# A threshold search on VectorE: one count with a sum, or a compare and a second compare that adds and sums

## The chip, the cores and the metric

The kernel runs on one core of a Trainium2 chip. The metric is device time in microseconds (us) of one execution; lower is better. The engines are named as the profile names them: PE is TensorE, DVE is VectorE, ACT is ScalarE, POOL is GpSimd, SP is SyncE.

## What is computed

One layer of a perceiver on 16 x 64 = 1024 tokens of width 1024: cross attention to 1601 context rows per batch entry, a gated feed-forward block that keeps only the larger half of its gate activations, and a small mixture of experts. The part that matters here is the middle one:

```python
def _L0_attn_ref(x, w_gate, w_up, w_down):
    s = jax.nn.silu(jnp.einsum('bsh,ih->bsi', x, w_gate))
    B, S, I = s.shape                       # I = 2752
    k = int(K_FACTOR * I)                   # 1376
    _, idx = jax.lax.top_k(-jnp.abs(s), k)
    flat = s.reshape(B * S, I)
    rows = jnp.arange(B * S)[:, None]
    flat = flat.at[rows, idx.reshape(B * S, k)].set(0.0)
    s = flat.reshape(B, S, I)
    s = s * jnp.einsum('bsh,ih->bsi', x, w_up)
    return jnp.einsum('bsi,hi->bsh', s, w_down)
...
x = x + _L0_xattn_ref(_layernorm(x, axis=-1), ctx_1024, ctx_1024, 0, mask_SxS2_ff0)
x = x + _L0_attn_ref(_layernorm(x, axis=-1), L0_attn_w_gate, L0_attn_w_up, L0_attn_w_down)
x = x + _L0_ffn_ref(_layernorm(x, axis=-1), ...)
```

In every token's row of 2752 gate values the 1376 of least magnitude are set to zero, the earliest ones where magnitudes are equal.

## The kernel before

The 1024 tokens are eight tiles of 128 rows (partitions). Attention comes first and takes about half of the time. GpSimd uses it to form sums of weight blocks for the feed-forward block, whose three matrix products are done for two tiles at a time, in a form with seven block products in place of eight (Strassen's way).

The feed-forward block works on four pairs of tiles. For pair n there is a gate projection (`widen` with k = 0, group g0 to g3), an up projection (`widen` with k = 1, u0 to u3) and a down projection (`down`, d0 to d3). Each unit of `widen` is eight PE matmuls into one of five PSUM banks; DVE and ACT add the products out of PSUM (evictions), and for the up projection POOL multiplies the result into the gate's rows `s` (tiles `v_u` in the profile). In `down`, POOL forms the sums of blocks of `s` that the seven products need (`S<-s`, `s<-s,s`, `s<-S,s`).

Between gate and down projection stands the selection, `drop_small`. It takes the magnitudes `a[0]` and `a[1]` of the pair's two tiles and finds for each row, bit by bit from bit 30 down, the threshold below which 1376 values lie. A float's bits, for positive numbers, order like the number, so the candidate threshold is built as an integer. Each of the 31 steps has three tasks:

- `below`, on DVE: for tile 0 of the pair, how many of 2752 magnitudes are under the candidate, less 1376, into `over[:, 0]`. It is one instruction, a compare whose accumulator starts at -1376. Its elementwise output `junk0` (2752 bytes a row) is not used in the search.
- `signs`, on ACT: for tile 1 of the pair, the sum of the signs of candidate minus magnitude, into `over[:, 1]`.
- `settle`, on DVE: two instructions on 128 x 2 values, `marks` and `cand`, which take the tried bit back where at least 1376 values were under it, and set the next.

After the last step come the ranks of equal values (a compare into `junk0`, then a scan, per half row and tile), the mask (`keep`, a three-operand instruction written into `rank`) and, on POOL, the multiplication of `s` by the mask (`zero`, in the profile `s<-s,rank`, 128 x 688). It needs the up projection's columns as well. Then PE turns the rows (`turned`, in the profile `ptd`) and the down projection starts. The magnitudes of the next pair are formed only when the pair before is done with `a`, so the four searches follow one another; and the up projection of a pair starts only when that pair's magnitudes exist.

The order of all this work is fixed when the program is built. Every piece is a task of `Plan`, with an engine, a cost in us, its dependences, a rank and the buffers that it takes. `Plan.run` plays the tasks in time with these costs and 0.1 us for a result that goes to another engine; whenever an engine is free it emits the ready task of lowest rank. The instructions of each engine then run in that order on the chip, whatever the real durations are. A task's cost is thus no limit on the chip, but it moves tasks of all engines in the order. The ranks of the projections on PE follow

```python
    order = ["g0", "u0", "g1", "g2", "d0", "u1", "g3", "d1", "u2", "d2", "u3", "d3"]
```

and in the search `below` and `signs` have rank 3, `settle` 1, evictions 0. Each step's tasks depend on the step before:

```python
            t0 = add("DVE", 3.15, below, [t], 3)
            t1 = add("ACT", 2.8, signs, [t], 3)
            t = add("DVE", 0.35, settle, [t0, t1], 1)
```

All recorded instructions carry the line of a helper (L93 in the profile), so the profile's groups are told apart by the names of tiles.

Of the kernel before, what the change touches and what calls it, by code (L numbers as in the profile page):

```python
# [9 lines left out]
F32 = mybir.dt.float32  # L10
I32 = mybir.dt.int32
BF16 = mybir.dt.bfloat16
# [4 lines left out]
ALU = mybir.AluOpType  # L17
# [13 lines left out]
I = 2752  # L31
# [11 lines left out]
WC = 3 * HC  # L43
GW, DW = NCC * (NH // 2) * IC, NB * HC
NU = 16
assert I % 2 == 0
K_ZERO = I // 2
E, R = 8, 16
SCALING = 8.0 / R
EPS = 1e-5  # L50
# [4 lines left out]
def tile_perceiver_layer(  # L55
# [41 lines left out]
    pe, dve, act = InOrder(nc.tensor), InOrder(nc.vector), InOrder(nc.scalar)  # L97
# [264 lines left out]
    def finish_tile(i, h, home=ps_t, tag="pt"):  # L362


        if h == 0:
            att[i] = xnp.tile([P, 2, 4, 4, HD], F32, tag="xn", name=f"att{i}")
        rows = att[i][:, h]
        pt = home.tile([P, 4, P], F32, tag=tag, name=f"pto{i}_{h}")
        for r in range(4):
            pe.transpose(  # L370
                pt[:, r, :], oT[i][:, h, r].rearrange("p b s -> p (b s)"), ident
            )

        def add():
            pool.tensor_tensor(
                rows, rows, rs_tok[i][:, h].unsqueeze(3).to_broadcast([P, 4, 4, HD]),
                ALU.mult,
            )
            xv = x[i].rearrange("p (h g r d) -> p h r g d", h=2, g=4, r=4)
            pool.tensor_tensor(xv[:, h], xv[:, h], rows, ALU.add)  # L380

        return (rows, pt.rearrange("p r (g d) -> p r g d", g=4)), add
# [35 lines left out]
    for n in range(ng):  # L418
# [11 lines left out]
        for d in range(2):  # L430
            add = None
# [6 lines left out]
            if n > 8 and 3 <= 2 * m + d <= 4:  # L438
                copy, add = finish_tile(i - 2, 1 - d)
# [93 lines left out]
    add = plan.add  # L533
    s, hS, held_h, hs, a, marked = {}, {}, {}, {}, {}, {0: [], 1: []}
# [232 lines left out]
    def drop_small(pair, n, gated, after, up):  # L767
# [10 lines left out]
        box = {}  # L778
# [18 lines left out]
        t = add("DVE", 4.4, magnitudes, gated[pair[0]] + gated[pair[1]] + after, 1)  # L797
        upped = up([t])
        for bit in range(30, -1, -1):

            def below():
                dve.tensor_scalar(
                    box["junk0"], a[0], box["cand"][:, 0:1].bitcast(F32),
                    float(-K_ZERO), ALU.is_lt, ALU.add,
                    accum_out=box["over"][:, 0:1],
                )

            def signs():
                act.activation(
                    box["sign1"], a[1], AF.Sign, bias=box["cand"][:, 1:2].bitcast(F32),  # L810
                    scale=-1.0, accum_out=box["over"][:, 1:2],
                )

            def settle(bit=bit):

                gone = marks[:, 2 * bit : 2 * bit + 2]
                dve.tensor_scalar(
                    gone, box["over"], 0.0, float(1 << bit), ALU.is_ge, ALU.mult
                )
                cand = small.tile([P, 2], I32, tag="cand", name=f"cand{n}_{bit}")  # L820
                dve.scalar_tensor_tensor(
                    cand, box["cand"], (1 << bit) >> 1, gone,
                    ALU.bitwise_or, ALU.bitwise_xor,
                )
                box["cand"] = cand
                box["over"] = small.tile([P, 2], F32, tag="over", name=f"over{n}_{bit}")

            t0 = add("DVE", 3.15, below, [t], 3)
            t1 = add("ACT", 2.8, signs, [t], 3)
            t = add("DVE", 0.35, settle, [t0, t1], 1)  # L830

# [15 lines left out]
        def one_short():  # L847
# [3 lines left out]
            dve.tensor_scalar(  # L851
                step, box["unequal"], box["trial"], float(2 * (I - K_ZERO)),
                ALU.subtract, ALU.is_gt,
# [11 lines left out]
        for j, i in enumerate(pair):  # L865
# [33 lines left out]
            t = [t] + [ts1] * j + marked[j]  # L899
            for h in range(2):  # L900
                t = [add("DVE", 5.5 if j else 4.0, lambda h=h, f=ranks: f(h), t, 2)]
            t = add("DVE", 0.6, limits, t + [tb[j]], 2)
            for h in range(2):
                t = add("DVE", 1.75, lambda h=h, f=keep: f(h), [t], 2)
# [334 lines left out]
    t = add("PE", 2.9, lambda: groups[-1].values(0, NTC), [], rank["g0"] - 5)  # L1239
    t = add("ACT", 0.3, lambda: groups[-1].keep(), [t], 0)  # L1240
# [23 lines left out]
    t = add("DVE", 1.3, sum_blocks, [over], rank["g1"], margin=30.0)  # L1264
    t = add("PE", 0.25, sum_rows, [t], rank["g0"], takes=held_ra)
# [4 lines left out]
    for n, pair in enumerate(pairs):  # L1270
        kept, t = drop_small(
            pair, n, gated[n], chosen,
            lambda t: widen(1, n, pair, rank[f"u{n}"], f"u{n}", lambda p: t, t),
        )
        chosen = [t]
        turns = turned(pair, rank[f"d{n}"] - 1, kept)
        downed = down(pair, n, rank[f"d{n}"], turns)
        for i in pair:
            ends[i] = experts(i, downed[i])
        if n == 0:  # L1280
            gated.append(
                gate(pairs[3], 3, rank["g3"], lambda i: ends[i - 6])
            )
# [3 lines left out]
class Plan:  # L1287
# [20 lines left out]
    def add(self, engine, cost, emit, deps, rank, takes=None, frees=None, margin=0.0):  # L1308
        holds, frees = (
            [hold for hold in (h if isinstance(h, tuple) else (h,)) if hold]  # L1310
            for h in (takes, frees)
        )
        task = self.Task(engine, cost, emit, deps, rank, holds, margin)
        for hold in frees:
            hold.freed_by = task
        self.tasks.append(task)
        return task
# [98 lines left out]
```

## Time and profile before

| what | value |
|---|---|
| three runs | 1718.9, 1718.66 and 1722.92 us, median 1718.9 |
| profiled execution, span from first to last instruction | 1719.5 us (no time of it outside the span is recorded) |
| PE busy | 1694.0 us, 99% of the span |
| DVE busy | 1413.0 us, 82% |
| ACT busy | 1259.6 us, 73% |
| POOL busy | 557.2 us, 32% |
| mean granted PE clock | 0.995 |
| `below` (junk<-a,cand, 128 x 2752) | 124 instances, mean 3078 ns, 381.7 us |
| `signs` (sign<-a,cand, 128 x 2752) | 136 instances (12 outside the steps), mean 2587 ns, 351.9 us |
| `marks` and `cand` of `settle` | 124 each, 157 ns |
| the four searches, first count to last settle | 920.9 to 1053.9, 1093.6 to 1228.7, 1271.2 to 1399.4, 1448.0 to 1579.8 us |

A line of the profile's groups names the engine, the operation, output <- inputs by the program's names, the shapes, how many instances there are, and their times. A timeline's line begins with the start and the duration in us; brackets at its end give the time for which the engine was idle before it and what ended that. Engines run beside each other, so busy shares do not add up.

### The profile page before, as it was taken

The page shows a single profiled execution, that of the slowest core. Times are in us where ns is not written, and L with a number is a line of the kernel's source. Part 1 is how long each engine was busy: PE and PEld are TensorE (multiplying, and loading weights), DVE is VectorE, ACT ScalarE, POOL GpSimd, SP SyncE. Part 2 cuts the span into 40 slices and gives each one's busy share as a digit, 9 for nine tenths or more (in the row PEclk, how much of TensorE's full clock was granted, in tenths as well). Part 3 has the DMA queues.
Part 4 walks back from the last instruction along what each step waited for, and adds up shares of the span by engine and source line. Part 5 has one row for each costly group of instructions (what it writes and reads, how often), then busy time and mean ns, then how long its engine had stood idle before and what let it go on. Part 6 is the DMA issues. An engine that isn't in the chain of part 4 may idle for free. (4 is left out here: it accounts for less than half of the span.)

```text
span 1719.5 us, 38732 instructions
## 1 busy us (share of the span) xinstructions
PE 1694.0 (99%) x15102; PEld 1152.2 (67%) x15102; DVE 1413.0 (82%) x3655; ACT 1259.6 (73%) x1780; POOL 557.2 (32%) x584
## 2 busy tenths in 40 slices
PE   8999999999999999999999999999989999999999
PEld 6777777777777777777766666655645646645644
DVE  7888888888888888888627999999999989999703
ACT  5999999999999999999544676577657782778010
POOL 2045454454444454110120211222282013331631
PEclk9999999999999999999999999999999999999999
DMA  8246456555556646121499999988969978888984
GB/s 248 74 122 207 148 194 210 188 166 195 170 185 206 204 159 208 57 75 58 182 349 324 308 292 304 302 267 291 324 202 292 309 251 301 283 294 270 316 265 143
DMA packets 132327, 384.56 MB, mean 224 GB/s; under 512 B 9489, under 2 KB 61233, under 8 KB 132145
## 3 DMA queue, kind: packets, MB, share of 16 engines
q1 hardware_dynamic: 113280, 312.83, 55.5%
q0 software_dynamic: 18432, 68.16, 12.1%
q8 instruction: 120, 1.97, 0.5%
q10 hardware_dynamic: 432, 1.09, 0.2%
q14 instruction: 63, 0.51, 0.1%
HBM read 339.58 MB, written 42.47 MB: 222 GB/s over the span
## 5 line engine op out<-in xcount | busy, mean ns | idle before, releaser
L93 DVE CUSTOM_DVE_ANT_0 sc<-ps,mask 128x512 f32<-128x512 f32 (+2 forms) x1024 | 526.4, 571 | 104.8 <-PE ps L93 104.4
L93 ACT ACTIVATE sign<-a,cand 128x2752 int8<-128x2752 f32 x136 | 351.9, 2587 | 110.9 <-DVE cand L93 110.5
L93 ACT ACTIVATE sc<-sc,nm 128x1601 f32<-128x1601 f32 x256 | 420.2, 1667 | 11.5 <-DVE nm L93 11.5
L93 PEld LDWEIGHTS pt<-ident,sc 128*128 128x128 f32 (+1 forms) x3328 | 361.9, 141 | 77.3 <-issue 72.8
L93 PE MATMUL pt<-ident,sc 128*128 128x128 f32 (+1 forms) x3328 | 391.1, 274 | 1.0 <-ACT sc L93 0.9
L93 DVE TENSOR_SCALAR_CACHE_REDUCE junk<-a,cand 128x2752 uint8<-128x2752 f32 x124 | 381.7, 3078 | 4.0
L93 ACT COPY pT<-pt 128x512 f32<-128x512 f32 x636 | 323.9, 609 | 46.5 <-PE pt L93 46.2
L93 PE MATMUL pg_g<-w_g,hS 128*128 128x344 f32 x896 | 261.2, 453 | 2.6 <-DMA w_g<-ts 1.8
L93 PE MATMUL pg_u<-w_u,hS 128*128 128x344 f32 x896 | 263.4, 452 | 0.0
L93 POOL TENSOR_TENSOR tw<-tw 128x344 f32<-128x344 f32 (+1 forms) x192 | 175.9, 927 | 265.5 <-DMA tw<-in_wg_dram 87.3
L93 PE MATMUL ps<-kT,qt 32*128 32x512 f32 (+2 forms) x2048 | 248.1, 550 | 4.6 <-DMA kT<-in_ctx_t_dram 3.4
L93 PE MATMUL pd<-w_d,s 128*128 128x512 f32 x528 | 235.2, 599 | 0.0
L93 PEld LDWEIGHTS pg_g<-w_g,hS 128*128 128x128 f32 x896 | 169.5, 190 | 91.0 <-issue 3.3
L93 PEld LDWEIGHTS pg_u<-w_u,hS 128*128 128x128 f32 x896 | 168.8, 190 | 87.4 <-issue 3.4
L93 PE MATMUL po<-pT,v 128*32 128x128 f32 x6656 | 208.2, 274 | 0.4 <-ACT oT L93 0.4
L93 PEld LDWEIGHTS po<-pT,v 128*32 128x32 f32 x6656 | 174.1, 110 | 48.6 <-issue 45.7
L93 PEld LDWEIGHTS pd<-w_d,s 128*128 128x128 f32 x528 | 99.9, 193 | 115.7 <-issue 114.6
L93 DVE COPY pT<-pt 65x128 f32<-65x128 f32 (+1 forms) x388 | 141.0, 418 | 22.9 <-PE pt L93 16.0
L93 PEld LDWEIGHTS ps<-kT,qt 32*128 32x128 f32 x2048 | 83.3, 184 | 53.9 <-DVE mx L93 36.7
L93 ACT ACTIVATE s<-s 128x344 f32<-128x344 f32 (+1 forms) x70 | 36.6, 535 | 74.8 <-DVE s L93 74.7
L93 POOL TENSOR_TENSOR s<-s,rank 128x688 f32<-128x688 f32 x32 | 62.4, 1965 | 77.3 <-DVE rank L93 76.7
L93 DVE DVE_READ_ACCUMULATOR2_ANT mx<- 128x1 f32 x1024 | 84.0, 82 | 0.0
(322 smaller groups left out, 1216.6 us busy)
## 6 DMA issues: line engine op xcount, KB each, us to landing
w_g<-ts SPq DMA_DIRECT2D x64, 688.0 KB
w_u<-ts SPq DMA_DIRECT2D x64, 688.0 KB
w_d<-ts SPq DMA_DIRECT2D x48, 768.0 KB
w_g<-in_wg_dram SPq DMA_DIRECT2D x48, 688.0 KB
w_u<-in_wu_dram SPq DMA_DIRECT2D x48, 688.0 KB
w_d<-in_wd_dram SPq DMA_DIRECT2D x36, 768.0 KB
kT<-in_ctx_t_dram SPq DMA_DIRECT2D x31, 800.5 KB
v<-in_ctx_v_dram SPq DMA_DIRECT2D x32, 768.0 KB
```

The costliest lines, as they stand in the source:

```text
L93: return tc.keep_in_program_order(getattr(self.engine, op)(*args, **kwargs))
```

## The change

The count of `below` becomes two instructions. The first compares the upper 1376 columns of `a[0]` with the candidate and adds -1, so that it writes 0 or -1 for each; it writes 16-bit values (the same bytes `junk0`, seen as 1376 values of bf16) and has no sum. The second compares the lower 1376 columns, adds the first one's output element by element, and sums: the sum is the number of magnitudes under the candidate less 1376, as before. The cost that `Plan` reckons for the task goes from 3.15 to 2.65. The rest of the search, `signs` and `settle` among it, stays.

```diff
-assert I % 2 == 0
 K_ZERO = I // 2
+assert K_ZERO == I - I // 2
...
         for bit in range(30, -1, -1):
 
             def below():
+                half, cand = I // 2, box["cand"][:, 0:1].bitcast(F32)
+                less = box["junk0"].bitcast(BF16)
                 dve.tensor_scalar(
-                    box["junk0"], a[0], box["cand"][:, 0:1].bitcast(F32),
-                    float(-K_ZERO), ALU.is_lt, ALU.add,
+                    less, a[0][:, half:], cand, -1.0, ALU.is_lt, ALU.add
+                )
+                dve.scalar_tensor_tensor(
+                    less, a[0][:, :half], cand, less, ALU.is_lt, ALU.add,
                     accum_out=box["over"][:, 0:1],
                 )
...
-            t0 = add("DVE", 3.15, below, [t], 3)
+            t0 = add("DVE", 2.65, below, [t], 3)
             t1 = add("ACT", 2.8, signs, [t], 3)
             t = add("DVE", 0.35, settle, [t0, t1], 1)
```

## The prediction

> **What bounds the kernel now.** I read the first two parts of the page first, then the busy time by stretch, one step of the search in order of time, the durations of the operations like the new ones, and the places where GpSimd and VectorE meet.
>
> ```profile
> span 1719.5 us, 38732 instructions
> ...
> PE 1694.0 (99%) x15102; PEld 1152.2 (67%) x15102; DVE 1413.0 (82%) x3655; ACT 1259.6 (73%) x1780; POOL 557.2 (32%) x584
> ```
>
> TensorE is busy for 99% of the span: whatever the search gains, only TensorE's idle time can be given back. Busy time by stretch (the four searches, first to last step, then the start of the second down projection; columns: stretch, its length, then PE, PEld, DVE, ACT and POOL busy, granted clock, DMA share, GB/s):
>
> ```profile
> 920.90:1053.90 133.00, 133.00 (x471) 87.78 (x470) 128.48 (x180) 94.31 (x91) 19.52 (x20) 1.00 0.96 306
> 1093.60:1228.70 135.10, 134.31 (x442) 75.56 (x441) 128.08 (x188) 100.59 (x102) 28.44 (x35) 1.00 0.86 287
> 1271.20:1399.40 128.20, 124.26 (x391) 70.87 (x390) 121.15 (x161) 99.38 (x98) 28.59 (x29) 0.99 0.85 275
> 1448.00:1579.80 131.80, 130.65 (x424) 72.71 (x423) 125.11 (x175) 96.76 (x92) 42.08 (x44) 1.00 0.86 289
> 1256.00:1292.00 36.00, 29.55 (x107) 16.24 (x106) 32.55 (x35) 24.66 (x32) 29.92 (x26) 0.91 0.53 170
> ```
>
> VectorE is 94 to 97% busy in every search, and the searches follow one another with only their ranking between, so VectorE's chain from 921 to about 1618 is a second, nearly full line beside TensorE. The one place where it visibly holds TensorE is the last row: from 1256 to 1292 TensorE idles 6.45 us and the clock falls to 0.91. The up projection of tiles 2 and 3 is over, nothing else is ready, and the turned rows of the down projection need the second search's result. In TensorE's timeline six down matmuls take 4.79 us there against 2.74 elsewhere, some 2 us more: about 8.4 us can be had.
>
> One step of a search, undisturbed (timeline):
>
> ```profile
> 1308.77 3.08 DVE L93 TENSOR_SCALAR_CACHE_REDUCE junk<-a,cand 128x2752 uint8<-128x2752 f32 x1
> 1308.83 2.59 ACT L93 ACTIVATE sign<-a,cand 128x2752 int8<-128x2752 f32 x1 [0.90 <-DVE cand L93]
> ...
> 1311.32 0.19 ACT L93 ACTIVATION_READ_ACCUMULATOR sign<-a,cand 128x1 f32 x1
> 1311.77 0.08 DVE L93 DVE_READ_ACCUMULATOR junk<-a,cand 128x1 f32 x1
> 1311.96 0.16 DVE L93 TENSOR_SCALAR marks<-over 128x2 int32<-128x2 f32 x1
> ...
> 1312.35 3.08 DVE L93 TENSOR_SCALAR_CACHE_REDUCE junk<-a,cand 128x2752 uint8<-128x2752 f32 x1
> ```
>
> The count ends at +3.08, its sum is out by then, the marks start at +3.19 and the next count at +3.58. ScalarE's half is out at +2.74, 0.45 before them: VectorE's count sets the step.
>
> **The new step.** Minimum, median and maximum durations in ns, from the views of single tiles:
>
> ```profile
> L93 DVE TENSOR_SCALAR_CACHE_REDUCE junk<-a,cand x124: 3069/3079/3081, 921.4 to 1574.3; 128x2752 uint8<-128x2752 f32 x124
> L93 DVE TENSOR_SCALAR junk<-a,cand x16: 927/936/2025, 1054.0 to 1606.2; 128x1376 uint8<-128x1376 f32 x16
> ...
> L93 DVE SCALAR_TENSOR_TENSOR rank<-rank,ties,sign x16: 1641/1652/2450, 1066.0 to 1616.0; 128x1376 bf16<-128x1376 int16 x16
> ...
> L93 POOL TENSOR_TENSOR s<-s,rank x32: 1482/1496/4207, 1069.3 to 1633.2; 128x688 f32<-128x688 f32 x32
> ```
>
> The compare of the upper half is the second row with a 16-bit output: same input, scalar and length, so 0.93 us. The second operation is nearest to the third row: 1376 elements, two tensors, a scalar per row, 1.64 us; a sum is read out inside the last 0.08 us of the old count, and I take the same here. Between two VectorE operations of which the second reads the first lie 0.03 us (a compare ends at 1230.17, its scan starts at 1230.20). The new count ends at 0.93 + 0.03 + 1.64 = +2.60, and VectorE could start the marks at +2.71. ScalarE's sum is out at +2.74, and where the marks wait for it they start 0.03 later (1284.43 to 1284.46): +2.77. So ScalarE, just, sets the new step, and the next count starts 0.39 later: 3.16 in place of 3.58. The step wins 0.42 where ScalarE ends last, and 3.08 - 2.60 = 0.48 where evictions lie between count and marks. At 0.45: 31 x 0.45 = 14.0 us for each search, 55.8 for the four. That is the change's whole gain, in VectorE's time and not yet in the span's.
>
> **What it adds.** Of the rows above, the old count never varies: 3069 to 3081 ns over 124 instances, though GpSimd is busy for 118.6 us (19.5 + 28.4 + 28.6 + 42.1) under them, and GpSimd's multiplications under it stay at 0.92 us. The two kinds that replace it do vary, and so does GpSimd beside them:
>
> ```profile
> 1243.84 1.64 DVE L93 SCALAR_TENSOR_TENSOR rank<-rank,ties,sign 128x1376 bf16<-128x1376 int16 x1
> 1244.00 2.26 POOL L93 TENSOR_TENSOR s<-s,v_u_(2, 1)_16238 128x344 f32<-128x344 f32 x1 [2.78 <-DVE v_u_(2, 1)_16238 L93]
> ...
> 1245.83 1.17 DVE L93 TENSOR_SCALAR junk<-a,cand 128x1376 uint8<-128x1376 f32 x1
> ...
> 1246.22 2.12 POOL L93 TENSOR_TENSOR s<-s,rank 128x688 f32<-128x688 f32 x1
> ...
> 1247.03 4.19 DVE L93 TENSOR_TENSOR_SCAN rank<-junk 128x1376 int16<-128x1376 uint8 x1
> ```
>
> GpSimd's 0.92 us multiplication starts at 1244.00 under the three-operand step and takes 2.26, ending where the step's end (1245.48) plus 0.8 lies; the compare behind it takes 1.17 for 0.93, and the scan 4.19 for 3.02. They take turns, whole instruction by whole instruction. So in the new search, where such operations fill 2.6 of 3.2 us, each GpSimd operation costs VectorE time that the old count did not lose.
>
> The price: where GpSimd works in a chain (the sums of the down projection, 1.0 us each), a step becomes 0.93 + 1.0 + 1.64 + 1.0 = 4.57 us, the second turn covering sum, marks and candidate: 1.41 over 3.16 for 2.0 us of GpSimd work, 0.7 per us. A single multiplication starts 0.08 after its eviction, while the next count would start 0.21 to 0.29 after that: 0.62 to 0.70 lost of 0.92, less where a second eviction follows. Chains of 1.27 or 1.5 us lose 0.8 per us. I take 0.7; the ends are 0.3 (most turns fall into the 0.55 us of each step between the sum's operation and the next compare) and 1.0 (every turn serial). Per search, cost against 14.0: 13.7, 19.9, 20.0 and 29.5. Net of the first +0.3, then -5.9, -6.0, -15.5.
>
> The Trainium skill's page "SBUF — State Buffer", section "The single rule", says that VectorE and GpSimd share one port pair as an exclusive lock, held by a VectorE instruction with two SBUF inputs or in a two-port mode, and that a tensor_scalar that writes out its accumulator does not take it. Read to the letter (whoever is second waits for a whole instruction) that is the serial end, 118.6 lost against 55.8 won.
>
> **Where that ends in the span.** (1) The second search ends 5.6 us later, and TensorE, already idle at 1256 for it, idles that much longer: +6. (2) The third search starts under the second down projection's sums. TensorE takes the first two of these as they end (1281.94 + 1.00, matmul at 1282.99; 1285.05 + 1.01, matmul at 1286.11). At 2.28 us per operation instead of 1.0 the second is the fourth operation in line and ends near 1291 instead of 1286: +5. The other down projections in a search have their sums well ahead of use (in the third, 1509.5 for a matmul at 1518.7). (3) By the last ranking the chain is 27 us late. It ended at 1617.9, and the rows of tile 7 are wanted at 1632, about 12 us of slack after GpSimd's multiplication; TensorE itself is 11 late: 27 - 12 - 11 = +4. Sum +15.
>
> **The planner.** It reckons a step at 3.15 + 0.35 = 3.5; with 2.65 ScalarE's 2.8 and two hops of 0.1 set it: 3.35, or 0.5 less where evictions fill it. It thus puts the down projections 5 to 15 us earlier in TensorE's order per search. The first has a real lead of some 16 us (rows multiplied by 1095.6, first turn at 1111.8); the second has none, so an earlier place there only moves the same wait. I price this at nothing, and at up to 10 us if turned rows are queued in front of up matmuls that were ready. The new second operation waits for the compare; queued behind it on VectorE are the evictions of TensorE's five banks, 11.6 us of matmuls (5 x 2.32), which covers a count longer by a turn or two. Memory, DMAs, ScalarE's and SP's work are the same.
>
> The three runs' median (1718.9) is 0.6 under this execution's span, and no time around the span is shown; I add to the median: 1718.9 + 15 = 1734.
>
> **Rivals.** *The search does get ahead* (0.25). GpSimd's turns fall mostly into gaps, at 0.3 per us: the second search ends 28 - 14.4 = 13.6 us earlier, TensorE's 8.4 us at 1256 come back, and up to 2 of the stall at 1392: 1709 to 1711. For it: only 22% of the searches' time has GpSimd busy. Against: the multiplications start just ahead of the next compare. It decides once the price is under 28 / 48 = 0.58 per us. *Nothing visible* (0.10): gain and turns cancel in the first two searches, 1714 to 1724. *The sum halves the second operation's rate* (0.05): 1376 elements more at the (3.08 - 1.64) / 1376 = 1.05 ns that old count and third row differ by, 1.44 us, so the step is 0.96 over the old and VectorE loses 119 us beside the turns: 1800 or more. Against: the third row runs at 1.64. *Forecast, slower* (0.60): 1725 to 1758, the upper end at a price of 0.9 (second search 43 - 28 = 15 late, sums 7, last ranking 107 - 56 - 12 - 22 = 17: +39), or at 0.7 with badly placed turns. At 1.0 the same sum gives 1770.
>
> The page "Vector Engine (DVE) Microarchitecture Reference", section "Points that are easy to get wrong", says that this kind with two non-bf16 sources from SBUF runs at half rate; the third row, int16 and int8, runs in 1.64 us and does not show it.
>
> **The numbers.** A measurement of this kernel can tell some 0.3%, 5.2 us. Faster 0.25, same 0.10, slower 0.65. Range 1709 to 1758: it leaves out the half rate and the outer ends.
>
> **What would show it.** Right: compares of 0.93 at least but with maxima near 2 us, second operations from 1.64 to 2.6; GpSimd's multiplications in the searches near 2 us instead of 0.92; marks released by ScalarE in quiet steps of 3.16; the second search's end at or after 1229 and a longer gap behind the second up projection. Wrong: both new rows at their minimum throughout and the second search over by 1215, or a second operation near 3 us.

## The result, and the profile after

| | before | changed |
|---|---|---|
| median of the runs | 1718.97 us | 1749.03 us (1747.66 to 1750.06) |
| ratio | | 1.0163, 95% interval 1.0148 to 1.0178 |
| span of the profiled execution | 1719.5 us | 1748.2 us |
| mean granted PE clock | 0.995 | 0.991 |

The changed kernel is slower by 30 us. (The ratio stands with its interval and is not the quotient of the two medians, 1.0175; by the ratio the loss is 28 us. One execution further down, of the old count with the cost 3.35, took 2890 us at a granted clock of 0.56 and is left out of its run's median.) First the page's first two lines, span and busy time by engine:

```profile
span 1748.2 us, 38857 instructions
...
PE 1703.0 (97%) x15102; PEld 1155.3 (66%) x15102; DVE 1398.1 (80%) x3779; ACT 1260.6 (72%) x1780; POOL 613.5 (35%) x584
```

TensorE runs the same 15102 matmuls in 1703.0 us of busy time, 9.0 more than before; VectorE has 15 us less to do; GpSimd, with the same 584 instructions, is busy 56 us longer. TensorE's waits from 850 us on (who waited for what, us in total, how often, the longest):

```profile
PE pt_f L93 <- ACT s L93: 7.2, 2, 6.8
PE ptd L93 <- ACT s L93: 6.6, 5, 3.3
PE pd L93 <- POOL s L93: 6.2, 2, 3.3
PE pt_f L93 <- ACT hS L93: 5.0, 3, 2.3
PE pg_u L93 <- DVE u_u L93: 2.6, 2, 1.6
PE pg_g L93 <- DMA w_g<-ts: 2.2, 1, 2.2
```

With five smaller ones they sum to 32.7 us. Before, they summed to 12.8, of which the first two are:

```profile
PE ptd L93 <- ACT s L93: 3.8, 4, 2.1
PE pt_f L93 <- ACT s L93: 2.6, 1, 2.6
```

Over the whole span TensorE's time outside its busy time grew from 25.5 to 45.2 us; these 19.7 and the matmuls' added 9.0 make the 28.7 by which the span grew. Matmuls are longer where the clock falls: the eight turns behind the longest wait, of 6.76 us, took 1.97 us (1.04 for eight at 1290.06), and in the stretch around them, the last of these, the clock is 0.83 (the four searches, then the longest wait; columns as for the stretches before).

```profile
922.50:1047.50 125.00, 122.31 (x433) 80.35 (x432) 119.09 (x206) 92.39 (x87) 24.18 (x20) 1.00 0.93 299
1085.80:1211.90 126.10, 121.21 (x376) 66.37 (x375) 115.94 (x200) 99.78 (x99) 38.01 (x25) 0.97 0.82 265
1257.80:1390.60 132.80, 120.81 (x396) 70.68 (x395) 121.67 (x192) 101.62 (x100) 55.57 (x36) 0.96 0.78 253
1424.40:1563.80 139.40, 132.88 (x444) 77.17 (x443) 129.05 (x220) 98.47 (x95) 59.27 (x40) 0.99 0.81 267
1300.00:1320.00 20.00, 13.24 (x35) 6.67 (x34) 14.93 (x19) 12.83 (x13) 16.79 (x13) 0.83 0.57 185
```

The searches end earlier than before: the second one at 1211.9 instead of 1228.7, and the last at 1563.8 instead of 1579.8. A quiet step, in the timeline:

```profile
1162.88 0.94 DVE L93 TENSOR_SCALAR junk<-a,cand 128x1376 bf16<-128x1376 f32 x1
1162.94 2.59 ACT L93 ACTIVATE sign<-a,cand 128x2752 int8<-128x2752 f32 x1 [1.45 <-DVE cand L93]
...
1163.85 1.65 DVE L93 SCALAR_TENSOR_TENSOR junk<-a,cand,junk 128x1376 bf16<-128x1376 f32 x1
...
1165.43 0.08 DVE L93 DVE_READ_ACCUMULATOR junk<-a,cand,junk 128x1 f32 x1
1165.44 0.19 ACT L93 ACTIVATION_READ_ACCUMULATOR sign<-a,cand 128x1 f32 x1
1165.65 0.16 DVE L93 TENSOR_SCALAR marks<-over 128x2 int32<-128x2 f32 x1
...
1166.04 0.94 DVE L93 TENSOR_SCALAR junk<-a,cand 128x1376 bf16<-128x1376 f32 x1
```

It lasts 3.16 us. VectorE's sum is out at 1165.51 and ScalarE's at 1165.63; the marks follow 0.02 behind ScalarE's, which is thus, just, what they wait for (behind VectorE's sum alone they came 0.11 later in the profile before, 1311.85 to 1311.96). Over all instances the two operations look like this (minimum, median, maximum in ns, in the view of the tile; the first row also holds the 16 compares of the ranking):

```profile
L93 DVE TENSOR_SCALAR junk<-a,cand x140: 921/937/2017, 923.1 to 1586.1; 128x1376 bf16<-128x1376 f32 x124, 128x1376 uint8<-128x1376 f32 x16
L93 DVE SCALAR_TENSOR_TENSOR junk<-a,cand,junk x124: 1650/1652/2766, 924.0 to 1561.7; 128x1376 bf16<-128x1376 f32 x124
```

The means are 1110 and 1860; with the gap between them a count takes 3.01 us on the mean, against 2.61 undisturbed and 3.08 before. What stretches them stands in the timeline of the third search, where the second down projection runs:

```profile
1299.05 1.09 DVE L93 TENSOR_SCALAR junk<-a,cand 128x1376 bf16<-128x1376 f32 x1
...
1299.48 1.51 POOL L93 TENSOR_TENSOR s<-S,s 128x384 f32<-128x384 f32 x1
...
1300.17 2.27 DVE L93 SCALAR_TENSOR_TENSOR junk<-a,cand,junk 128x1376 bf16<-128x1376 f32 x1
...
1300.95 3.93 POOL L93 TENSOR_TENSOR S<-s 128x384 f32<-128x384 f32 x2
...
1313.22 2.26 DVE L93 SCALAR_TENSOR_TENSOR junk<-a,cand,junk 128x1376 bf16<-128x1376 f32 x1
1314.12 1.41 POOL L93 TENSOR_SCALAR ve_f<-sq_f 128x1 f32<-128x1 f32 x1
...
1316.25 0.19 POOL L93 TENSOR_TENSOR shift_f<-minus_f,rstd_f 128x1 f32<-128x1 f32 x1
...
1316.47 1.24 ACT L93 ACTIVATE s<-s,shift_f,rstd_f 128x1024 f32<-128x1024 f32 x1 [6.33 <-POOL shift_f L93]
...
1317.77 1.97 PE L93 MATMUL pt_f<-ident,s 128*128 128x128 f32 x8 [6.76 <-ACT s L93]
```

GpSimd's sums, 1.0 us each before, stretch over nearly 2, VectorE's second operation to 2.27. A layer norm's small steps (`ve_f`, `shift_f`) stand behind those sums in GpSimd's queue, ScalarE's scaling waits 6.33 us for them, and TensorE, whose queue holds that tile's turns next, 6.76. In the profile before TensorE's longest wait for such a step was 2.61 us, although ScalarE waited 12.78 for GpSimd's small steps there (to 1260.26): how long TensorE waits depends also on what its queue holds next.

### The profile page after: what moved, and what is told of

Read it like the earlier page. It is cut to its first block, busy times and chain, and to the rows that moved or that the text cites. A ratio compares the mean times of both kernels' runs of the same rounds, so it can differ in the third digit from the quotient of the medians.

```text
span 1748.2 us, 38857 instructions
## 1 busy us (share of the span) xinstructions
PE 1703.0 (97%) x15102; PEld 1155.3 (66%) x15102; DVE 1398.1 (80%) x3779; ACT 1260.6 (72%) x1780; POOL 613.5 (35%) x584
## 3 DMA queue, kind: packets, MB, share of 16 engines
q0 software_dynamic: 18432, 68.16, 11.8%
q8 instruction: 120, 1.97, 0.5%
## 5 line engine op out<-in xcount | busy, mean ns | idle before, releaser
L93 DVE SCALAR_TENSOR_TENSOR junk<-a,cand,junk 128x1376 bf16<-128x1376 f32 x124 | 230.6, 1860 | 4.4
L93 DVE TENSOR_SCALAR junk<-a,cand 128x1376 bf16<-128x1376 f32 (+1 forms) x140 | 156.3, 1116 | 4.0
```

The lines of the kernel that those rows point to most:

```text
L93: return tc.keep_in_program_order(getattr(self.engine, op)(*args, **kwargs))
```

## The experiments

Two explanations stood against each other. **A:** GpSimd and VectorE block each other in the two new operations, and TensorE waits for what comes late. **B:** the cost of 2.65 changes the order on every engine, and that order puts work into TensorE's queue before its inputs are there. The edit has both in it, so I took them apart: three counts in two orders.

**The new instructions in the old order.**

```diff
-            t0 = add("DVE", 2.65, below, [t], 3)
+            t0 = add("DVE", 3.15, below, [t], 3)
```

> The changed instructions with the planner's old cost of 3.15, so that every engine runs in the order of the kernel before. Theory A (GpSimd and VectorE block each other in the two new operations, and TensorE waits for GpSimd's results): still slow, 1735 to 1750 us, GpSimd's busy time near the 613 us of the changed kernel. Theory B (the planner's order for 2.65 puts turns and other work in front of TensorE before their inputs are there): the loss goes with the order, 1710 to 1722 us.

Measured: 1723.87 us, ratio to before 1.0024 (1.0014 to 1.0034). GpSimd's busy time is 631 us, more than in the changed kernel, and yet most of the loss is gone. A's number is missed, and B's by 2 us. By themselves the instructions cost 4 us, and the other 25 go with the order.

**The old count in the new order.**

```diff
-            t0 = add("DVE", 3.15, below, [t], 3)
+            t0 = add("DVE", 2.65, below, [t], 3)
```

> The old count with the planner's cost set to 2.65: the order of the changed kernel, with a count that never shares. Theory A: 1715 to 1728 us, GpSimd's busy time stays near 557. Theory B: 1740 to 1755 us, at least as slow as the changed kernel, since the old count is 0.48 us longer than the new one and the order is the same.

Measured: 1749.23 us, 1.0169 (1.0154 to 1.0184), as slow as the changed kernel without one shared turn in the search: its count stays at 3064 to 3081 ns and GpSimd at 552 us. TensorE's waits in this run from 850 us on, the first five:

```profile
PE ptd L93 <- ACT s L93: 8.3, 5, 3.7
PE pd L93 <- POOL s L93: 4.1, 2, 2.5
PE pt_f L93 <- ACT hS L93: 3.5, 3, 1.3
PE pg_g L93 <- DVE s L93: 3.2, 5, 1.2
PE pt_m L93 <- DVE xd L93: 2.8, 3, 1.7
```

The same kinds of work are waited for, in smaller pieces and now also for VectorE itself. The searches end early here too, the second at 1218.3 and the last at 1562.2: it is mainly the order that moves them, not the new count. So far B holds. But is the order bad, or is the count late for it? The next two runs ask that with a count that is short and never shares; it leaves 448 columns of tile 0 out of the search.

**A short count with a sum, in both orders** (the first with 2.65, the second with 3.15).

```diff
-                    box["junk0"], a[0], box["cand"][:, 0:1].bitcast(F32),
+                    box["junk0"][:, :2304], a[0][:, :2304], box["cand"][:, 0:1].bitcast(F32),
```

> One count with a sum over the first 2304 of the 2752 columns (448 columns are left out of tile 0's count), cost 2.65: as long as the two new operations undisturbed, 2.61 us, same order as the changed kernel, but one tensor and no two-port mode. Theory A: 1705 to 1720 us, faster than before by what the shorter count wins. Theory B: 1735 to 1750, like the changed kernel.

> The same short count (448 columns of tile 0 left out) with the cost 3.15, the order of the kernel before. Both theories: TensorE's idle time at 1256 comes back, 1708 to 1714 us. If VectorE's chain does not hold TensorE anywhere: 1718 to 1720. The difference to the changed instructions in the same order is the price of sharing alone.

Measured: 1705.72 us in the new order, 0.992 (0.9905 to 0.9934), and 1712.08 in the old, 0.9957 (0.994 to 0.9973). B's number for the new order is missed by 30 us, and A's is met: that order is the better one, by 6 us, if the count takes the 2.61 us that it was reckoned from. In the old order the range was met but not its reason: of TensorE's waits behind 1256, 2.61 and 2.13 us, 1.99 and 1.81 stayed, and the gain is spread over the whole search. In the new order TensorE waits for nothing to speak of; from 850 us on:

```profile
PE pg_g L93 <- DMA w_g<-ts: 1.5, 1, 1.5
PE ptd L93 <- ACT s L93: 1.2, 4, 0.6
PE ph L93 <- DVE den L93: 0.4, 1, 0.4
PE py L93 <- ACT hwT L93: 0.4, 1, 0.4
```

Neither A nor B stands alone. The three counts in two orders, medians in us:

| count | undisturbed / mean length | old order (3.15) | new order (2.65) |
|---|---|---|---|
| old, one sum | 3.08 / 3.08 | 1720.1 | 1749.2 |
| changed | 2.61 / 2.97 in the old order, 3.01 in the new | 1723.9 | 1749.0 |
| short, never shares | 2.61 / 2.61 | 1712.1 | 1705.7 |

(The median of before was 1720.1 on the chip of these runs, and 1719.0 on that of the changed kernel.) In the old order the sharing takes 11.8 us and the shorter count gives 8.1. In the new order the sharing takes 43.3, and the shorter count gives 43.5.

Why the prices depend so much on the order can be read from where the last search ends. Its last instruction is the last `cand`, which starts at the end of the range in these rows. The old order, with the old, the changed and the short count:

```profile
L93 DVE SCALAR_TENSOR_TENSOR cand<-cand,marks x124: 156/157/159, 925.0 to 1579.7; 128x2 int32<-128x2 int32 x124
L93 DVE SCALAR_TENSOR_TENSOR cand<-cand,marks x124: 156/157/158, 925.0 to 1582.8; 128x2 int32<-128x2 int32 x124
L93 DVE SCALAR_TENSOR_TENSOR cand<-cand,marks x124: 156/157/158, 923.3 to 1569.8; 128x2 int32<-128x2 int32 x124
```

The new order, in the same sequence:

```profile
L93 DVE SCALAR_TENSOR_TENSOR cand<-cand,marks x124: 156/157/158, 923.9 to 1562.1; 128x2 int32<-128x2 int32 x124
L93 DVE SCALAR_TENSOR_TENSOR cand<-cand,marks x124: 156/157/158, 926.2 to 1563.7; 128x2 int32<-128x2 int32 x124
L93 DVE SCALAR_TENSOR_TENSOR cand<-cand,marks x124: 156/157/158, 924.0 to 1519.8; 128x2 int32<-128x2 int32 x124
```

| count | old order: the four searches, last end, rest of the span | new order |
|---|---|---|
| old, one sum | 528.7, 1579.8, 139.7 us | 524.6, 1562.2, 184.4 us |
| changed | 530.1, 1582.9, 139.6 | 523.3, 1563.8, 184.4 |
| short, never shares | 518.1, 1569.9, 139.6 | 480.3, 1519.9, 183.6 |

What follows the last search takes 139.6 or 139.7 us in the old order and 183.6 to 184.4 in the new one, whatever the count. The new order leaves some 130 more of TensorE's matmuls for that time (587 to 598 recorded, against 460 to 462). It pays only if the last search ends 44 to 45 us earlier in return: with the short count it ends 50 earlier, with the old and the changed count 18 and 19, and the rest is the loss. In the old order even the short count takes only 10.6 us from the four searches, where 124 x 0.47 would be 58. With the old count TensorE was already busy for 522.7 of the 528.7 us of these searches, so there is little to take, and VectorE, whose busy time in them falls from 503.3 to 449.8 us, waits instead. In the new order there is more: TensorE is busy for 497.3 of 524.6 us with the old count and for 479.5 of 480.3 with the short one. In the old order, between 920 and 1600 us, VectorE's two longest waits with the short count are for ScalarE's sums and the down projection's matmuls (5.0 and 1.8 us with the old count):

```profile
DVE marks L93 <- ACT sign L93: 17.8, 48, 2.7
DVE xd L93 <- PE pd L93: 13.6, 9, 2.8
```

**How late is late: two more lengths in the new order.** As the short count, with 2528 and 2648 columns.

> As the short count, cost 2.65, with 2528 columns (224 columns of tile 0 left out): 2.84 us, half way between the 2.61 of the short count (1705.7 us) and the 3.08 of the whole one (1749.2), all in one order and none sharing. If lateness against the order is what costs, a value between: about 1727 us on a straight line. If a threshold is crossed: near one of the two ends.

> The same with 2648 columns (104 of tile 0 left out): 2.97 us, the mean that the two changed operations and their gap took in the changed kernel. If the changed kernel's loss is the mean length of its count alone: 1749, like it. If GpSimd's own delay in taking turns adds to it: less, about 1739 on the straight line.

Measured: 1722.25 us (ratio 0.9999, 0.9989 to 1.0008) and 1736.37 us (1.0087, 1.0072 to 1.0102), 5 and 3 us under the straight line. With the ends that makes four lengths in one order: 2.61, 2.84, 2.97 and 3.08 us give 1705.7, 1722.3, 1736.4 and 1749.2. Per us of count length the slopes are 72, 108 and 116, or by the ratios, since the middle two ran on another chip, some 60, 120 and 130; there are 124 counts. The four searches take 480.3, 497.9, 513.4 and 524.6 us, and 183.3 to 184.4 follow the last one. So in this order most of the time by which the counts are late comes out at the end, in the old order (8.1 us for 0.47) only 17 us per us. The changed kernel lies 12.7 above the third value. My length for it left out the gap between the two operations: at 3.01 in place of 2.97 some 4 us of these are length too (0.036 x 116). In the two traces the first search begins 3.7 us later in the changed kernel (922.5 for 918.8), which is not the count's doing, and the searches take 9.9 longer, these 4 among them. That the other 6 belong to GpSimd's own results coming late and to turns that bunch is likely from the waits shown above, but was not isolated.

**Which of the two operations shares.** All with 2.65; first the compare alone stays as changed:

```diff
-                dve.scalar_tensor_tensor(
-                    less, a[0][:, :half], cand, less, ALU.is_lt, ALU.add,
-                    accum_out=box["over"][:, 0:1],
+                dve.tensor_scalar(
+                    box["junk0"][:, :half], a[0][:, :half], cand, float(-K_ZERO),
+                    ALU.is_lt, ALU.add, accum_out=box["over"][:, 0:1],
                 )
```

> Cost 2.65. The changed kernel's first compare stays (two-port mode, 16-bit output, its result unused); the second operation is a count with a sum of the lower half alone, one tensor, which never shares (the upper half is left out of tile 0's count). As long as the changed count undisturbed. If the second, two-tensor operation carries the sharing (it fills 1.65 of the 2.6 us): 1706 to 1720 us. If the compare does: 1738 to 1750. If by their measured excess (0.18 and 0.21 us a step): 1718 to 1735.

Then the second operation alone:

```diff
+            dve.memset(box["junk0"].bitcast(I32), 0)
...
+                scrap = small.tile([P, 1], F32, tag="scrap", name="scrap")
                 dve.tensor_scalar(
-                    less, a[0][:, half:], cand, -1.0, ALU.is_lt, ALU.add
+                    less[:, :693], a[0][:, half : half + 693], cand, -1.0,
+                    ALU.is_lt, ALU.add, accum_out=scrap,
                 )
```

> Cost 2.65. The changed kernel's second operation stays; the compare before it becomes one with a sum over 693 columns, 0.93 us, one tensor and no two-port mode (683 columns of the upper half are left out of tile 0's count, and each search clears the 16-bit buffer once, 0.8 us). If the second operation carries the sharing: 1738 to 1752 us. If the compare does: 1708 to 1720. If both by their excess: 1722 to 1738.

Measured: 1717.84 us (0.9983, 0.9974 to 0.9993) and 1723.72 us (1.0017, 1.0007 to 1.0026), that is 12 and 18 over the short count's 1705.7. Their groups of instructions (busy us, mean ns):

```profile
L93 DVE TENSOR_SCALAR_CACHE_REDUCE junk<-a,cand 128x1376 uint8<-128x1376 f32 x124 | 204.1, 1646 | 4.4
L93 DVE TENSOR_SCALAR junk<-a,cand 128x1376 bf16<-128x1376 f32 x124 | 137.6, 1110 | 3.9
```

```profile
L93 DVE SCALAR_TENSOR_TENSOR junk<-a,cand,junk 128x1376 bf16<-128x1376 f32 x124 | 219.8, 1772 | 4.5
L93 DVE TENSOR_SCALAR_CACHE_REDUCE junk<-a,cand 128x693 bf16<-128x693 f32 x124 | 116.0, 936 | 3.9
```

The forms with one tensor and a sum keep their undisturbed length (1646 and 936), the compare without a sum and the two-tensor operation do not. Both share, as the range for both in f3 says; f2 lies just below its range for both and inside the one for the second operation alone. The two losses make 30 of the 43 us, and the rest appears only when both share. The counts are 2.79 and 2.75 us long there, and the searches, 492.8 and 493.4 us, take about what the lengths without sharing would give (494 and 491, by a line between 2.61 and 2.84). The 0.63 us of clearing per search puts 2.5 us into the second run.

**Is any other cost as bad?** The new and the old count with 3.0, then with 3.35.

> The changed instructions with the cost 3.0, near the 2.97 us that the two operations took on the mean in the changed kernel. If the loss comes from an order that expects the count earlier than it comes: 1712 to 1724 us, no worse than with 3.15. If the cost only shuffles the order by chance: anything from 1710 to 1750.

> The old count, 3.08 us, with the cost 3.0: 0.15 under the cost of before, 0.08 under what it takes. If the loss with 2.65 comes from an order that expects the count too early, a third of the step at most: 1718 to 1730 us. If any other order than that of before is bad by chance: up to 1750.

> The old count with the cost 3.35, so that the order expects the count 0.27 us later than it comes. If the order loses only where it expects too much, 1714 to 1726 us, as with 3.15. If 3.15 is good by chance and every other order loses: 1728 to 1750.

> The changed instructions with the cost 3.35. If the order loses only where it expects too much: 1714 to 1726 us, as with 3.15 or a little better, since the two operations took 2.97 on the mean. If 3.15 is good by chance: 1728 to 1750.

| cost | old count | ratio to before | changed count | ratio to before |
|---|---|---|---|---|
| 2.65 | 1749.2 | 1.0169 (1.0154 to 1.0184) | 1749.0 | 1.0163 (1.0148 to 1.0178) |
| 3.0 | 1731.8 | 1.0065 (1.0050 to 1.0080) | 1735.7 | 1.0088 (1.0073 to 1.0103) |
| 3.15 | 1720.1 | 1 | 1723.9 | 1.0024 (1.0014 to 1.0034) |
| 3.35 | 1727.4 | 1.0034 (1.0022 to 1.0047) | 1732.6 | 1.0064 (1.0048 to 1.0081) |

All four expectations of lateness were missed: 3.0 cost more than I thought, and 3.35 cost something too. The ranges for chance, with any other order than that of 3.15 losing, were met in three of the four, and the old count with 3.35 lies 1 us below its own. The rest of the span behind the last search shows what the cost moves: it is 184.4 us with 2.65, 167.2 and 167.6 with 3.0 (old and changed count), 139.7 with 3.15 and 124.1 with 3.35 (changed count). With 3.0 the last search ends 15.2 and 13.9 us earlier than with 3.15, not the 28 that are added behind it. With 3.35 there are 15.5 us less behind it, but it ends 25.6 later (1608.5 for 1582.9), its searches being longer; why they are stays open, and 3.15 may simply be a good order among several. Of the kernels that count all columns none was faster than before.

## Why the prediction was right or wrong

The direction and the range held: 1734 was forecast, 1749 came, inside 1709 to 1758. The sum behind it did not hold, and that the direction was right is luck: of the loss, 25 us come from the planner's order, which the sum put at nothing, and 4 from the instructions, for which it had 15. Its terms are held here against e1, the run of the new instructions in the order for which they were reckoned; in the changed kernel the order moves the searches as well.

- **The new step** was right. 3.16 us was worked out and 3.16 is what quiet steps take, with the marks at +2.77 behind ScalarE's sum. Both undisturbed durations were right to 0.01 us.
- **The gain, 55.8 us of VectorE's time**, failed. It took every step to be as long as VectorE's work in it. In the old order the short count, which loses nothing to GpSimd, shortened the four searches by 10.6 us in all, because TensorE was busy for nearly all of them already and VectorE then waits. In the new order the same count gave 44.3.
- **The turns** were right in kind and too dear. The price was 0.7 us per us of GpSimd's work. It measured (2.97 - 2.61) x 124 = 45 us over the 118.6 us of that work, 0.38, and in the changed kernel 50 us, 0.42. In a chain the step is not 4.57 but 3.90 us (1299.05 to 1302.95): VectorE's second operation grows by 0.62, and after it come 0.51 us without a shared turn and 0.16 more in the compare, not a whole GpSimd instruction of 1.0 each time. I had taken the duration that the profile shows for GpSimd's instruction as the time in which it keeps VectorE out. Of the 45 us, only 12 are in the searches' length (530.1 for 518.1).
- **The second search 5.6 us later, +6**: in e1 it ends at 1227.7, 1.0 earlier than before, so gain and turns cancelled and the term is 0. In the changed kernel it ended 16.8 us earlier, and my sign for a wrong forecast, over by 1215, came true in its second half; but with the old count in the same order it was already over at 1218.3.
- **The sums of the second down projection, +5**: GpSimd's sums did take 1.3 to 1.7 us on the mean instead of 0.93. In e1 TensorE came to this stretch 1.6 us earlier than before (matmuls at 1276.09 for 1277.65) and left it 2.4 later (1288.53 for 1286.11), 4.0 in all, near the term, but by another way. The wait for the first sum only went from 0.64 to 1.16 us; turns ahead of it waited too, and six matmuls behind it took 4.93 us instead of 2.84, at a clock of 0.57 from 1283.4 to 1288.5 where it had been 1.00. By 1396 TensorE was 1.6 us ahead again.
- **The last ranking, +4**: the chain was to be 27 us late. In e1 the ranking ended 3.0 us later than before (1620.9 for 1617.9), and the span grew by 3.1: the size is near, but neither the 27 nor the 12 us of slack taken off it were there. In the changed kernel it ended at 1594.5, and with the old count in that order at 1592.9.
- **The planner at nothing, 10 at most** is the step that failed most. It measured 1749.0 - 1723.9 = 25 us with the changed instructions and 29 with the old ones. I had seen that the cost moves the down projections earlier in TensorE's order, and took an earlier place for harmless because the wait would only move. But the order for 2.65 leaves 44 to 45 us more of work behind the last search, which fits a count of 2.61 us; a longer one costs some 60 to 130 us per us of its length.
- **The rivals.** What the instructions alone did, 1723.9, is the case *nothing visible*, in which gain and turns cancel (1714 to 1724). *The search does get ahead* had its price, 0.38 being under its turning point of 0.58, and yet in that order the four searches took 530.1 us for 528.7: the gain that the price was set against was not there. The short count's 1712.1 is near this rival's 1709 to 1711, but not by TensorE's idle time at 1256, most of which stayed.
- **The half rate** did not show: 1376 elements of fp32 and bf16 took 1.65 us.

The lock of the Trainium skill's page "SBUF — State Buffer", section "Who interferes with whom" ("The single rule"), agrees with these runs in which forms share: the tensor_scalar with a sum never varied (3064 to 3081 ns in e2), the one without a sum and the two-tensor form did. Its whole-instruction reading does not agree with the durations that the profile shows: a sum of 1.0 us kept the second operation out for 0.62 us, and VectorE lost 45 to 50 us to GpSimd's 118.6, not all of them.

## What to carry to other kernels

Before an instruction is traded for two shorter ones, compare not only their undisturbed durations but what they share: a form with one tensor and a sum was immune to GpSimd here, and the pair that was 0.47 us shorter kept 0.07 of it (0.11 in the old order). Where an order is written out from costs, a cost is a promise to every queue: this one was worked out from undisturbed durations, and the same order gave 1705.7 us with a count that kept it and 1749 with two that did not. A cost near the mean length that sharing leaves, 3.0, was no cure: it lost 12 us against 3.15. Look at what an order leaves behind the last link of the chain, and whether that link can end as early as the order needs. Change the instruction and the order's cost in separate runs, for neither of them tells its price in the other's company (the sharing cost 12 us in one order and 43 in the other).

## What the runs showed of the hardware

- GpSimd's smallest instructions wait for a turn like large ones: `ve_f`, one element per row, took 1.41 us under VectorE's second operation and ended 0.05 after it (1315.53 and 1315.48), against 0.19 before.
- A GpSimd instruction keeps VectorE's next operation out for less time than it is shown to last: 0.62 us in the chain at 1300, where its sums of 384 columns last 1.0 us undisturbed.
- A 16-bit output made the compare no faster than an 8-bit one: minimum and median are 926 and 937 ns over the changed kernel's 124, against 927 and 936 over the 16 before, for 1376 columns.
